# A fused two-layer graph network on one core: four edits at the seams between its stages

## The chip, the cores and the metric

The kernel runs on one core of a Trainium2 chip. A core has a matrix engine (TensorE, PE in the profile; its weight loads are PEld), a vector engine (VectorE, DVE), a scalar engine (ScalarE, ACT), a general engine (GpSimd, POOL), and SyncE (SP), which here issues almost all transfers between main memory and the on-chip memory. Each engine works through its own list of instructions in order; semaphores hold it back until what it reads is there. The metric is the device time in microseconds. Three runs of the kernel before took 2126.36, 2128.33 and 2132.01 us; the median, 2128.33 us, is the time before.

## The reference

There are 64 graphs of 256 nodes with 256 features, each with an adjacency matrix. Two layers follow each other, both with a layer norm and a ReLU at their input and a residual sum at their output.

```python
# layer 0
adj_hat = adj + eye; d = sum(adj_hat) ** -0.5
x = x + relu((d * adj_hat * d) @ h @ W.T + b)          # h = relu(layernorm(x))
# layer 1, h = relu(layernorm(x)) again
c = relu(bn1(conv1(h)))                                # 1 tap: a product with a 256 x 256 matrix
x_conv = relu(bn2(conv2(c)) + h)                       # 17 taps along the nodes
s = h @ w_se.T + b_se                                  # 3 columns
A = exp(-|s_n - s_m|^2) * adj
x_nmp = A @ relu(h @ w_msg.T + b_msg)
r, z, n = GRU gates of (concat(x_conv, x_nmp), h)
x = x + (1 - z) * n + z * h
```

All values are 32-bit floats.

## The kernel before

**Stage one** is a loop over n = 0 .. 67, software-pipelined over the 64 graphs: in pass n it aggregates and projects graph n (`aggregate`, `project`: layer 0), turns the normed rows of graph n-2 (`turn_h`), makes its messages (`messages`) and its first convolution (`conv1`), turns the three columns of graph n-3 (`turn_cols`) and computes its `distance`, and passes the messages of graph n-4 (`pass_messages`). Loads of `x` and `adj` come for two graphs at a time. Between these PE steps stands `beat(us)`: it runs the evictions and element-wise steps that are due (`after(k, ...)` puts a step off by k beats) and issues paced work of the long convolution, so much per microsecond of PE work. The wrappers `pe`, `act`, `vec` and `pool` keep the written order on these four engines. Transfers on SP are ordered by the scheduler and can be issued earlier than they are written.

In the profile, tiles are named: `ag`/`aggT` aggregation, `o`/`pre`/`x` projection and layer 0's sum, `ht`/`h2T` turned rows, `ms`/`mso`/`cols` messages and columns, `c`/`c1o` first convolution, `st`/`L`/`R`, `di`/`e`/`aT` distance and its mask, `nm`/`xnT` passed messages. `st` on DVE are moments of rows.

**Items.** Extra PE work is spread over the loop by `item()`, called up to eight times a pass. `pace` is a pair: what a call adds, and the credit it starts from; an item runs when the credit reaches 1. The 17-tap convolution is done with spectra: 48-point transforms of windows of the nodes, products per frequency, inverse transforms. First come its **filters**: at the end of pass 8 the turned taps are loaded into tiles `tp` (`filter_load`), and 32 items (`filter_part`) each make four products `fs` of 17 rows and 72 columns, in four banks of the PSUM memory, on four strips of 32 rows of the array; they are evicted to `fo` and stored as `wfd`. While filters run, only two of the eight calls count (`item(True)`), so two sets run a pass. When the list is empty, `conv_start` begins the convolution of the first 16 graphs: 32 `spectrum` items (`df` in the profile), then 24 `product` items (`y`), and the inverse transforms as paced work on POOL, DVE and ACT (`Xf`, `scr`, `hr`).

**Stage two** begins after the loop. PSUM is handed out anew: banks `ta`, `tc` and two `n` are first written by a product of the identity with a bias row `brzB`, so that later products add to what is there; then ACT copies the real biases in (`bank_of`). For each group q of 16 graphs, `turn_outputs` turns the convolution's outputs (`yt`, evicted to `xcT`), the spectra of the next group are computed (`spectrum`, which loads its next tile `h1l`), and then `gates` works on one graph after the other, with the `product`s of the next group between its parts. `wf_load` fetches the filters of one frequency part to one of eight tiles `wf` (WF = 8).

The lines that the change touches:

```python
            if 2 <= n <= B + 1:
                conv1(n - 2)
...
                    pace[:] = FILTER / 2, -5.0
...
    for tag, bufs in (("ta", 1), ("tc", 1), ("n", 2)):
        for k in range(bufs):
            t = ps_gate.tile([P, 2 * D], FP, tag=tag, name=f"first_{tag}_{k}", bufs=bufs)
            pe.matmul(t, ident, brzB, start=True, stop=True)
```

Of the kernel before, what the change touches and what calls it, by code (L numbers as in the profile page):

```python
# [11 lines left out]
FP = mybir.dt.float32  # L12
# [173 lines left out]
def gnn_kernel(  # L186
# [10 lines left out]
    B, N, D = x.shape  # L197
    P = 128
# [5 lines left out]
    NG = 16  # L204
# [6 lines left out]
    def scratch(name, shape):  # L211
# [17 lines left out]
    ident = const.tile([P, P], FP, tag="ident", name="ident")  # L229
# [4 lines left out]
    brzB = const.tile([P, 2 * D], FP, tag="brzB", name="brzB")  # L234
# [6 lines left out]
    pe, act, vec, pool = (  # L241
        Pinned(tc, e) for e in (nc.tensor, nc.scalar, nc.vector, nc.gpsimd)
    )
# [3 lines left out]
    def after(beats, go):  # L247
        due.append([beats, go])

    def come_due():  # L250
        now = []
        for d in list(due):
            d[0] -= 1
            if d[0] < 0:
                now.append(d[1])
                due.remove(d)
        for go in now:
            go()
# [59 lines left out]
    WF = 8  # L318

    def wf_load(n):  # L320
        if n < len(PARTS):
            u, k = PARTS[n]
            cv.wf[n] = wf = cv.stream.tile(
                [P, DC, D], FP, tag="wf", name=f"wf_{cv.q}_{u}_{k}", bufs=WF
            )
            nc.sync.dma_start(wf, wf_d[3 * u + k].rearrange("(c p) d -> p c d", c=DC))
# [217 lines left out]
    with ExitStack() as one:  # L544
# [11 lines left out]
        def beat(us):  # L556
            come_due()
            paced.issue(*(k * us for k in share))
# [442 lines left out]
        def own_bank(tag, k, bias):  # L1001
            width = bias.shape[2]
            shape = [P, NB, 512] if tag == "ms" else [P, NB, D]
            own[tag] = t = ps_own.tile(shape, FP, tag=tag, name=f"{tag}_{k}")
            act.copy(t[:, :, :width], bias.broadcast_to([P, NB, width]))

        def to_rows(g, tag, wT):
            s, t = st[g], own.pop(tag)
            for nb in range(NB):
                for cc in range(DC):  # L1010
                    pe.matmul(
                        t[:, nb, : wT.shape[2]], s["hT"][:, cc, nb * P : (nb + 1) * P],
                        wT[:, cc, :], start=False, stop=(cc == DC - 1), skip_group_check=True,
                    )
            return t

        def conv1(g):
            t = to_rows(g, "c1", w1T)

            def keep():  # L1020
                h1 = work.tile([P, NB, D], FP, tag="c1", name=f"c1o_{g}")
                act.activation(h1, t, AF.Relu)
                nc.sync.dma_start(h1_d[g].rearrange("p (c d) -> p c d", c=NB), h1)
            after(1, keep)
            if g + 1 < B:
                after(2, lambda: own_bank("c1", g + 1, b1B))
# [90 lines left out]
        t = ps_own.tile([P, NB, 512], FP, tag="ms", name="first_ms")  # L1117
        for nb in range(NB):
            pe.matmul(t[:, nb, :], ident, full, start=True, stop=True)
        t = ps_own.tile([P, NB, D], FP, tag="c1", name="first_c1")  # L1120
# [18 lines left out]
        pace = [0.0, 0.0]  # L1139
# [35 lines left out]
        FILTER, SPECTRA, PRODUCTS = 2, 5, 3  # L1175
        filtering = []
        for n in range(B + 4):
            even, odd = n % G == 0, n % G == 1
            if filtering and not items:
                filtering.clear()  # L1180
                while due:
                    beat(0.0)
                conv_start()
            if even and n + 2 * G < B:
                after(3, lambda n=n: load(n + 2 * G))
            if 2 <= n <= B + 1:
                turn_h(n - 2)
            beat(0.4)
            item()
            if n < B:  # L1190
                aggregate(n)
                if odd and n + 1 < B and n > 0:
                    after(2, lambda n=n: factors(n + 1))
                    for r in range(NR):
                        after((5, 7, 8, 9)[r], lambda r=r, n=n: layer0_in(n + 1, (r,)))
                if even and n + G < B:
                    after(4, lambda n=n: degrees(n + G))
                if odd and n + 3 < B:
                    for r in (0, 2):
                        after(3 + r // 2, lambda r=r, n=n: row_moments(n + 3, (r, r + 1)))  # L1200
            beat(1.7)
            item()
            if 3 <= n <= B + 2:
                turn_cols(n - 3)
            beat(0.2)
            if n + 1 < B:
                turn_adj(n + 1)
            beat(0.4)
            item()
            if n >= 4:  # L1210
                pass_messages(n - 4)
            beat(1.7)
            item(True)
            if 2 <= n <= B + 1:
                messages(n - 2)
            beat(1.7)
            item()
            if 3 <= n <= B + 2:
                distance(n - 3)
            beat(0.6)  # L1220
            item()
            if n < B:
                project(n)
            beat(1.7)
            item(True)
            if 2 <= n <= B + 1:
                conv1(n - 2)
            beat(1.7)
            item()
            if n == 0:  # L1230
                small_turns()
                turn_part(wmT, nat_wm, 0, D, "wm")
                T(WI, 0)()
                L(WI, 4)()
                own_bank("ms", 0, bmB)
            if n == 1:
                small_shift()
                turn_part(w1T, nat_w1, 0, D, "w1", scale=sc[:, 0:DC])
                beat(0.4)
                own_bank("c1", 0, b1B)  # L1240
                T(WI, 2)()
                L(WH, 0)()
            if n >= 2 and later:
                for go in later.pop(0):
                    go()
                if not later:
                    while due:
                        beat(0.0)
                    prep_stack.close()
                    spec_stack = ExitStack()  # L1250
                    spec = spec_stack.enter_context(tc.tile_pool(name="spec", bufs=1))
                    tab = spec.tile([P, 3 * UNITS], FP, tag="tab", name="tab")
                    nc.sync.dma_start(tab, nc.inline_tensor(filter_table(), name="tab_c").ap())
                    tp = {k: filter_load(k) for k in range(2)}
                    filtering.append(True)
                    pace[:] = FILTER / 2, -5.0
                    items.extend(
                        lambda k=k, j=j: filter_part(k, j) for k in range(4) for j in range(QC // 8)
                    )
# [8 lines left out]
    ps_gate = ctx.enter_context(tc.tile_pool(name="ps_gate", bufs=2, space=PSUM))  # L1268
# [222 lines left out]

    LEAD, PER = 3, 6

    for tag, bufs in (("ta", 1), ("tc", 1), ("n", 2)):
        for k in range(bufs):
            t = ps_gate.tile([P, 2 * D], FP, tag=tag, name=f"first_{tag}_{k}", bufs=bufs)
            pe.matmul(t, ident, brzB, start=True, stop=True)
    ready["ta"], ready["tc"] = bank_of("ta"), bank_of("tc")
    for nb in range(NB):
        ready["n", nb] = bank_of("n")  # L1500
# [1 line left out]
    for q in range(1, GROUPS + 1):  # L1502
        share[:] = 0.6, 0.6, 0.3
        ld = gate_inputs(q - 1, 0)
        paced.drain()
        xcT = big.tile([P, DC, P, OUT], FP, tag="xcT", name=f"xcT_{q}")
        turn_outputs(xcT)
        for go in gate_parts(ld, xcT):
            go()
        todo = []  # L1510
        if q < GROUPS:
            conv_begin(q)
            for k in range(WF):
                wf_load(k)
            for g in range(NG):
                for cb in range(DC):
                    spectrum(g, cb)
            for u in range(1, AHEAD):
                sums(u)
            todo = [lambda u=u: product(u) for u in range(UNITS)]  # L1520
            for _ in range(LEAD):
                todo.pop(0)()
        for g in range(NG):
            share[:] = (0.42, 0.55, 0.3) if todo else (0.51, 0.62, 0.3)
            between = [todo.pop(0) if todo else lambda: None for _ in range(PER)]
            ahead, nxt = None, None
            if g + 1 < NG:
                ahead = gate_inputs(q - 1, g + 1)
                nxt = gate_parts(ahead, xcT)
            gates(ld, between, nxt)  # L1530
            ld = ahead
            if q + 1 < GROUPS and g >= NG - H1:
                h1_load(q + 1, g - NG + H1)
# [34 lines left out]
```

## Time and profile before

| What | Value |
|---|---|
| median of three runs | 2128.33 us |
| profiled execution, its own time | 2127.08 us |
| its span, first to last instruction | 2125.3 us |
| PE busy | 2070.2 us, 97% of the span |
| DVE, ACT, POOL busy | 1415.8, 1018.1, 1098.4 us |
| mean granted clock of PE | 0.99 |
| first filter products | from 144.3 us |
| last product of stage one | 878.1 to 881.9 us |
| first turned outputs of stage two | 888.4 us |

The page's rows give an engine, an operation, its output and inputs by tile name, their shapes, a count, busy time and mean duration, and then the idle time of the engine ahead of these instructions with what ended it. Nearly all rows name line 102, which is the wrapper that records every operation, so rows are told apart by their tiles. In the view of waits, each line has the waiting engine and tile, what it waited for, and total, count and longest. In the timeline a line has start, duration, engine, operation, tiles, and in brackets the idle time before it. The clock is the share of full speed that PE was granted.

### The profile page before, as it was taken

Reading aid. Unit: us, or ns where it says so; the run is one execution under the profiler, and the core shown is the slowest. Engines: PE = TensorE matmul, PEld = TensorE weight load, DVE = VectorE, ACT = ScalarE, POOL = GpSimd, SP = SyncE. Lnnn points to the kernel's source line nnn. Section 1 sums busy time; section 2 is a strip of 40 time slices with the busy share of each in tenths; the row PEclk is TensorE's granted clock in tenths of the full one; section 3 lists DMA queues with packets and bytes.
Section 4 is the critical chain, followed back from the end, with each engine's and each line's share of the span. In section 5 each row is a group of like instructions: output and inputs, shape, how many; then the busy total and the mean of one; then the engine's idle time right before and its main releaser. Section 6 shows DMA issues by size and latency. Waiting matters only on the chain. (4 is left out here: it accounts for less than half of the span.)

```text
span 2125.3 us, 31287 instructions
## 1 busy us (share of the span) xinstructions
PE 2070.2 (97%) x9977; PEld 1741.0 (82%) x9977; DVE 1415.8 (67%) x3207; ACT 1018.1 (48%) x2203; POOL 1098.4 (52%) x1309
## 2 busy tenths in 40 slices
PE   7989999999999999999999999999999999999998
PEld 6866666888888888688888888888888888888887
DVE  6545656544588998515989924989933889964444
ACT  4856666666456676532234442233452234343333
POOL 4333323334675555327766716766725767644343
PEclk9999999999999999999999999999999999999999
DMA  8696777756766554556533446533355523322231
GB/s 289 229 250 213 226 221 231 260 174 187 238 214 211 181 173 156 178 177 194 169 105 113 136 149 198 184 109 111 113 155 180 176 85 123 112 81 92 90 100 60
DMA packets 292442, 352.86 MB, mean 166 GB/s; under 512 B 19475, under 2 KB 232102, under 8 KB 291622
## 3 DMA queue, kind: packets, MB, share of 16 engines
q1 hardware_dynamic: 291664, 346.26, 51.7%
q0 software_dynamic: 288, 4.46, 0.6%
q8 instruction: 80, 1.31, 0.3%
q14 instruction: 84, 0.69, 0.1%
q10 hardware_dynamic: 326, 0.14, 0.0%
HBM read 224.43 MB, written 126.35 MB: 165 GB/s over the span
## 5 line engine op out<-in xcount | busy, mean ns | idle before, releaser
L102 DVE TENSOR_TENSOR Xf<-y,k 128x256 f32<-128x256 f32 x184 | 69.1, 416 | 182.8 <-PE y L102 180.5
L102 DVE SCALAR_TENSOR_TENSOR Xf<-Xf 128x256 f32<-128x256 f32 (+1 forms) x248 | 183.9, 756 | 6.5 <-ACT Xf L102 5.4
L102 PE MATMUL ta<-T,S 128*128 128x256 f32 x768 | 186.6, 379 | 0.0
L102 PE MATMUL y<-wf,Xf 128*128 128x256 f32 x768 | 182.4, 380 | 1.7 <-DVE Xf L102 1.4
L102 POOL TENSOR_TENSOR aT<-e,adjT 128x512 f32<-128x512 f32 x64 | 82.3, 1286 | 187.3 <-ACT e L102 187.3
L102 POOL TENSOR_TENSOR rz<-u,p 128x256 f32<-128x256 f32 x64 | 47.8, 747 | 245.0 <-ACT u L102 245.0
L102 ACT ACTIVATE rz<-rz 128x512 f32<-128x512 f32 x128 | 80.2, 627 | 184.0 <-DVE rz L102 181.0
L102 PEld LDWEIGHTS y<-wf,Xf 128*128 128x128 f32 x768 | 144.4, 190 | 24.4 <-DVE Xf L102 2.6
L102 PEld LDWEIGHTS ta<-T,S 128*128 128x128 f32 x768 | 145.9, 190 | 19.8
L102 PE MATMUL n<-wiT,hx 128*128 128x256 f32 x512 | 152.3, 379 | 0.0
L102 DVE SCALAR_TENSOR_TENSOR h2l<-rz,h2l 128x256 f32<-128x256 f32 x128 | 104.4, 816 | 53.6 <-POOL h2l L102 53.6
L102 POOL TENSOR_TENSOR rs<-ve,mhalf 128x2 f32<-128x2 f32 (+1 forms) x65 | 46.9, 722 | 172.6 <-DVE nm L102 167.2
L102 POOL TENSOR_TENSOR xs<-Xf 128x256 f32<-128x256 f32 x92 | 70.9, 776 | 125.4 <-ACT Xf L102 63.4
L102 PE MATMUL o<-w0T,aggT 128*128 128x256 f32 x512 | 129.0, 395 | 5.6 <-ACT aggT L102 5.6
L102 POOL TENSOR_TENSOR adjH<-adjT,eye 128x512 f32<-128x512 f32 x64 | 82.0, 1282 | 96.5 <-ACT adjT L102 96.2
L102 PE MATMUL n<-whT,hx 128*128 128x256 f32 x512 | 131.4, 379 | 0.0
L102 PE MATMUL n<-wiT,xcT 128*128 128x256 f32 x512 | 131.4, 379 | 0.0
L102 PE MATMUL ms<-wmT,h2T 128*128 128x259 f32 x512 | 124.7, 386 | 2.8 <-DVE h2T L102 2.8
L102 PE MATMUL nm<-aT,mso 128*128 128x256 f32 x512 | 123.2, 384 | 4.2 <-POOL aT L102 3.4
L102 PE MATMUL ag<-adjH,hs 128*128 128x256 f32 x512 | 121.7, 380 | 4.8 <-POOL adjH L102 3.4
L102 PE MATMUL c<-w1T,h2T 128*128 128x256 f32 x512 | 125.9, 390 | 0.0
L102 PEld LDWEIGHTS o<-w0T,aggT 128*128 128x128 f32 x512 | 93.4, 192 | 35.8 <-issue 15.9
(185 smaller groups left out, 5339.3 us busy)
## 6 DMA issues: line engine op xcount, KB each, us to landing
wf<-wfd SPq DMA_DIRECT2D x284, 256.0 KB
wfd<-fo SPq DMA_DIRECT2D x32, 576.0 KB
x2d<-x SPq DMA_DIRECT2D x64, 256.0 KB
h2d<-h SPq DMA_DIRECT2D x64, 256.0 KB
hTd<-h2T SPq DMA_DIRECT2D x64, 256.0 KB
h1d<-c1o SPq DMA_DIRECT2D x64, 256.0 KB
xnd<-xnT SPq DMA_DIRECT2D x64, 256.0 KB
h1l<-h1d SPq DMA_DIRECT2D x64, 256.0 KB
```

The costliest lines, as they stand in the source:

```text
L102: return self.tc.keep_in_program_order(getattr(self.engine, op)(*args, **kwargs))
```

## The change

Four edits. The filter products start from a credit of -7 instead of -5, two calls later, which is one pass of the loop. The first convolution of the last graph (63) is made in pass 66, after the distance of that graph, instead of pass 65. The four gate banks are first written by four products of 32 rows of the identity, each on its own strip of the array, instead of four products with all 128 rows. In stage two the eight first filter tiles of a group are asked for beside the last eight spectra instead of ahead of all of them.

```diff
@@ stage one, pass n @@
-            if 2 <= n <= B + 1:
+            if 2 <= n <= B:
                 conv1(n - 2)
+            elif n == B + 2:
+                conv1(B - 1)
@@ start of the filters, end of pass 8 @@
-                    pace[:] = FILTER / 2, -5.0
+                    pace[:] = FILTER / 2, -7.0
@@ start of stage two @@
-    for tag, bufs in (("ta", 1), ("tc", 1), ("n", 2)):
-        for k in range(bufs):
-            t = ps_gate.tile([P, 2 * D], FP, tag=tag, name=f"first_{tag}_{k}", bufs=bufs)
-            pe.matmul(t, ident, brzB, start=True, stop=True)
+    for r, tag in enumerate(("ta", "tc", "n", "n")):
+        t = ps_gate.tile([P, 2 * D], FP, tag=tag, name=f"first_{r}", bufs=1 + (tag == "n"))
+        at = slice(32 * r, 32 * (r + 1))
+        pe.matmul(t, ident[at, :], brzB[at, :], start=True, stop=True)
@@ stage two, group q @@
-            for k in range(WF):
-                wf_load(k)
             for g in range(NG):
+                if g >= NG - WF:
+                    wf_load(g - NG + WF)
                 for cb in range(DC):
                     spectrum(g, cb)
```

## The prediction

> **What bounds the kernel now.** First the page: TensorE (PE) is busy for 97% of the span, so only its idle stretches and its slow stretches can be won.
>
> ```profile
> PE 2070.2 (97%) x9977; PEld 1741.0 (82%) x9977; DVE 1415.8 (67%) x3207; ACT 1018.1 (48%) x2203; POOL 1098.4 (52%) x1309
> ```
>
> Then the view of waits for PE (us in total, times, longest):
>
> ```profile
> PE fs L102 <- ACT e L102: 9.4, 1, 9.4
> ...
> PE nm L102 <- POOL aT L102: 3.4, 2, 3.0
> ...
> PE df L102 <- DMA h1l<-h1d: 1.4, 3, 0.9
> ...
> PE first_ta L102 <- ACT xnT L102: 0.7, 1, 0.7
> ```
>
> These four waits lie where the change works. The windows around them (us, busy time of PE, PEld, DVE, ACT, POOL, then granted clock, DMA share, GB/s) show that idleness is not the whole price: after it PE runs at half clock.
>
> ```profile
> 145.40:154.80 9.40, 0.01 (x2) 0.00 (x0) 3.64 (x15) 1.50 (x4) 0.00 (x0) 0.74 0.97 315
> 154.80:160.10 5.30, 5.25 (x11) 3.12 (x12) 3.10 (x10) 2.80 (x6) 2.28 (x3) 0.50 0.68 211
> ...
> 875.10:878.10 3.00, 0.00 (x0) 0.00 (x0) 2.90 (x4) 1.99 (x6) 2.30 (x4) 0.80 0.77 259
> 878.10:882.60 4.50, 3.78 (x8) 2.52 (x8) 3.72 (x6) 0.59 (x1) 3.31 (x3) 0.50 0.27 78
> 882.60:888.00 5.40, 5.37 (x8) 2.31 (x9) 0.00 (x0) 1.01 (x3) 0.01 (x1) 0.58 0.51 143
> ```
>
> Last, the timeline before the first filter products, to see who really is late:
>
> ```profile
> 139.78 0.39 SPq L822 DMA_DIRECT2D x<-in_x_dram  x1
> ...
> 144.33 1.08 PE L102 MATMUL fs<-tp,tab 17*72 17x512 f32 x4
> ...
> 150.92 0.43 DVE L102 BATCH_NORM_STATS2 st<-x 128x6 f32<-128x256 f32 x1 [13.10 <-DMA x<-in_x_dram]
> ...
> 153.07 0.16 DVE L102 COPY cols<-ms 128x24 f32<-128x24 f32 x1
> 153.26 0.60 ACT L102 ACTIVATE mso<-ms 128x512 f32<-128x512 f32 x1 [11.70 <-DVE cols L102]
> ...
> 154.42 0.65 ACT L102 ACTIVATE e<-di 128x256 f32<-128x256 f32 x2
> ...
> 154.85 2.25 PE L102 MATMUL fs<-tp,tab 17*72 17x512 f32 x4 [9.44 <-ACT e L102]
> 154.96 0.60 ACT L102 ACTIVATE hs<-x,nmr,rsd 128x256 f32<-128x256 f32 x1
> ```
>
> The filter products wait for PSUM banks that ACT's `e` must read out; ACT stands behind `mso`, `mso` behind DVE's `cols`, and `cols` behind the row moments of an `x` tile issued at 139.78 and there at 150.92. The tap tiles `tp` delay it: ten loads issued from 124.45 to 131.92, and DMA is 0.96 busy at 136 GB/s from 130 to 145.4.
>
> [...] a filter set, four products of 17 rows, holds PE for 1.02 to 1.05 us between `o` and `c`. [...] a DVE `Xf` of 256 columns takes 0.42 us alone and 1.48 beside a POOL sum. [...] `x` has a row of 0.39 us and 11.1 us until it is read.
>
> **Filters a graph later.** Up to 144.33 both programs are the same, the `x` and `tp` loads too, so `x` still lands at 150.9. PE now goes on with graph 11's `c` (1.8) and `ht` (0.4) to 146.6, and two of eight passes of `ag` of graph 12; the rest needs the second row block of `hs`. In the changed instruction order that stays behind `mso` and `e` on ACT: ready at 154.96 + 0.60 = 155.56. The wait moves to `ag` and is 9 us again. From 155.56 to 160.12 the clock is half as before: six passes of `ag` at 0.43 (2.56), `st` and `at` (0.65 x 2 = 1.3), 0.7 of `nm`. Then at full clock 1.4 of `nm`, `ms` 1.95, `di` 0.64, `o` 1.92, one filter set 1.1: the next `c` starts at 167.1, against 172.15 before, where three sets were done. Two sets are owed: one after `o` (1.02 + 0.09) and one after `nm` (1.61 + 0.09), 2.8 together. Gain 5.05 - 2.8 = 2.3 us. One 3.41 us clock window more or less at half rate is 1.7 either way: 0.6 to 4.0.
>
> The sets' evictions `fo` and stores `wfd` move with them and are still issued before the first convolution starts. The later end of the filters delays the start of the first convolution by a graph too. Its products are PE work of the same sum; its transforms on DVE, POOL and ACT end nearer to the end of stage one: after the last `h2T` copy DVE has three more 512-wide steps (3 x 0.70 = 2.1 us). Those are in the next sum.
>
> **The joint of the stages.** `c` of graph 63 stood at 870.16 and covers PE's wait for `aT` of graph 62 (POOL 871.15 + 1.27 = 872.42; `nm` starts at 872.48). Moved, that wait is bare (1.8 us idle) and `nm` starts no earlier; `c` then covers 1.75 us of the wait for `aT` 63. The move itself is worth 0; its eviction and its `h1d` store come some 5 us later, and only the last group reads them. But POOL's residual sums now stand behind `aT` 63, so it starts at 875.95, not at 876.64, and is not slowed: done at 877.2 (878.09 before). `nm` 63 takes 877.3 to 879.1 at full clock (878.13 to 881.9 before), and its copy `xnT` ends at 880.0 (882.6).
>
> The four bank-setting products hold PE from 882.63 to 888.40, mostly at half clock: 5.8 us. As row tiles, by the filter set's row, 1.0: 880.0 to 881.1. Most of that is not gained, because the outputs' turning (`yt`) comes next. Its evictions into `xcT` reuse stage one's memory and wait for the landing of graph 63's `xnd` store. Before, that store was issued at 883.57, and `whT`, which waits for it, at 886.69: 3.1 us. In the changed SP order the store stands behind the load `hr_4`, which needs the sums of point 7. I put those at 882.1: ACT's two 0.4 us products at 877.5, DVE held by POOL's sums to 880.6, 0.4, and a sum of 1.0. Store 882.7, landing 885.8, first eviction 885.9 against 889.12. PE, with three banks, idles from 882 to 886.6, so half clock for one window; the turning then takes its 7.1 us (889.12 to 896.23) plus about 1.3 (a pair of banks is 1.7 us of PE then, against 1.0 us of evictions). `df` starts at 894.3, not 896.23: gain 1.9; bounds -1 (two half-clock windows, `nm` slow as well) and 3.3 (no half clock).
>
> Costed at nothing there: on POOL the weight difference `T` of `whT` now stands ahead of point 15's last sum. `whT` goes out at 885.9, lands 4.6 later (886.69 to 891.26 before) at 890.5, then 0.73 and 0.97: 892.2. Its last transposes come near 893.4; past that it costs us for us. `hr_12` moves between `h1l` loads 4 and 5 on SP and waits for that sum; load 5 waits for a buffer until about 899 anyway.
>
> **Filter tiles after h1.** No gain. In both instruction orders of SP these eight loads stand in stage one for the first group, some 150 rows ahead of `h1l_3`, and 80 to 90 rows ahead in later groups: the scheduler had hoisted them already. Bounds: the `df` waits are 1.4 us in all, so 0 to 1.4; below zero little, as products follow 13 us after.
>
> **Sum.** Profiled execution 2127.08 (span 2125.3 and 1.8 around it), 1.25 below the median 2128.33. 2127.08 - 2.3 - 1.9 = 2122.9; as a median 2124.1.
>
> **Rivals.** (1) The first wait vanishes: 9.44 idle and 5.3 us at half clock (2.65), with the joint's 1.9: 2114.3. For it: the wait stands at `fs`. Against: `ag` reads `hs` from the same stuck ACT. (2) The gains cancel in clock windows and a slower turning: 2128. For: half clock costs 1.7 per window, and new idle stretches appear at the joint. Against: nothing longer than before. (3) Slower: with the convolution a graph later, DVE's transforms collide with `h2T`. Place: 600 to 870 us, where DVE is 87 and 92% busy in two 100 us windows and eight PE waits from 730 to 866 sum to 4.3 us, 0.53 each. If each of some 25 graphs there had one, 13.3 us: 2128.3 + 9.0 - 4.2 = 2133.1. It decides once DVE's work per graph exceeds PE's 10.6 us; counted in the changed order with the rows' durations it stays between 9.2 and 10.9, as before.
>
> **How the numbers follow.** My case 0.65, own range 2120 to 2128.5; rivals 0.13, 0.10, 0.12. The range 2117 to 2132 leaves out rival 1 and half of rival 3. 0.3% is 6.4 us, about what a measurement of this kernel can tell from no change. Faster by more: rival 1 and a tenth from my case, 0.23; slower 0.07; same 0.70.
>
> **What would show it.** DVE `st` waits about 13 us for `x` again, and a PE wait of about 9 us at `ag` near 146.6 to 155.6 replaces that at `fs`. If that wait is under 5 us, rival 1 is right. Four `first` products within 2 us; then an idle gap of 4 us or more ahead of the later `yt`; `df` starting 6 to 8 us after the first `xcT`. SP issues `wf` and `h1l` in the same order. I am wrong at the joint if `yt` follows the products without a gap.

## The result, and the profile after

The changed kernel took 2121.47 us (median of six runs, 2119.73 to 2122.24) against 2128.35 for the kernel before, run beside it: a ratio of 0.9965, 95% interval 0.9955 to 0.9976. That is 0.35% less, or 6.9 us; the forecast median was 2124.1. The profiled execution after has a span of 2120.1 us (before: 2125.3). The page's first part:

```profile
PE 2067.2 (98%) x9977; PEld 1741.6 (82%) x9977; DVE 1412.2 (67%) x3207; ACT 1017.8 (48%) x2203; POOL 1099.2 (52%) x1309
```

The view of waits for PE after the change (total us, times, longest):

```profile
PE ag L102 <- ACT hs L102: 9.1, 2, 8.7
...
PE yt L102 <- ACT xcT L102: 4.6, 4, 4.0
...
PE nm L102 <- POOL aT L102: 2.4, 3, 1.8
...
PE first L102 <- ACT xnT L102: 0.7, 1, 0.7
```

The wait of 9.4 us at `fs` is now one of 8.7 at `ag`. A wait of 4.0 us ahead of `yt` is new. A line that the same view had before is gone:

```profile
PE fs L102 <- DVE pre L102: 2.0, 2, 1.0
```

These are two waits of 1.0 us of filter products for a bank that DVE's `pre` had still to read. The windows around the new waits, after the change (us, busy time of PE, PEld, DVE, ACT, POOL, then granted clock, DMA share, GB/s):

```profile
147.15:155.80 8.65, 0.00 (x0) 0.00 (x1) 4.41 (x17) 2.32 (x6) 0.46 (x1) 0.74 0.89 312
155.80:161.60 5.80, 5.80 (x17) 4.80 (x18) 3.15 (x12) 4.69 (x10) 2.25 (x4) 0.50 0.70 222
864.94:868.14 3.20, 1.11 (x7) 0.50 (x7) 2.92 (x7) 1.82 (x5) 1.53 (x1) 1.00 0.15 58
868.14:871.56 3.42, 3.42 (x8) 2.53 (x8) 1.23 (x4) 0.00 (x0) 0.00 (x0) 0.50 0.00 0
...
877.37:878.44 1.07, 1.07 (x8) 0.31 (x8) 0.97 (x3) 0.57 (x2) 0.38 (x2) 1.00 0.52 131
878.44:883.92 5.48, 1.53 (x16) 1.29 (x12) 5.20 (x8) 3.11 (x8) 2.84 (x3) 1.00 0.52 174
883.92:888.60 4.68, 4.68 (x26) 4.52 (x27) 2.28 (x4) 2.08 (x4) 0.54 (x1) 0.64 1.03 362
```

The reader sees the four bank products in 1.07 us (5.77 before), then PE busy for 1.53 of 5.48 us, then `yt` partly at half clock (0.64 on the mean); and, new, `nm` of graph 62 wholly at half clock (0.50) after a stretch in which PE was idle for 2.09 of 3.20 us. The timeline before the first wait, after the change:

```profile
131.68 0.54 SPq L784 DMA_DIRECT2D tp<-wtd  x1
140.62 0.39 SPq L822 DMA_DIRECT2D x<-in_x_dram  x1
...
151.11 0.43 DVE L102 BATCH_NORM_STATS2 st<-x 128x6 f32<-128x256 f32 x1 [13.13 <-DMA x<-in_x_dram]
...
153.45 0.60 ACT L102 ACTIVATE mso<-ms 128x512 f32<-128x512 f32 x1 [11.74 <-DVE cols L102]
...
155.80 1.65 PE L102 MATMUL ag<-adjH,hs 128*128 128x256 f32 x3 [8.65 <-ACT hs L102]
```

`x` is as late as before, and the same chain stands behind it. Milestones, as start times on PE in the two traces, before minus after: `c` after the wait 4.31 us, with two filter sets owed (not yet made, but made by then before the change); `di` of graph 20, 9.40; `di` of graph 50, when everything owed is done, 6.70; `di` of graph 62, 4.59; the first `df` of stage two, 4.44; the end, 5.25. So the wait alone did not earn the gain (4.31 less 2.8 owed is 1.5), and the joint earned nothing. Between graphs 13 and 20 something else came in. The trace of before shows it. Its timeline at one filter set:

```profile
239.89 1.08 PE L102 MATMUL fs<-tp,tab 17*72 17x512 f32 x4
240.00 0.48 DVE L102 SCALAR_TENSOR_TENSOR pre<-o,dis,b0B 128x256 f32<-128x256 f32 x1 [1.83 <-PE o L102]
...
241.44 0.47 DVE L102 SCALAR_TENSOR_TENSOR pre<-o,dis,b0B 128x256 f32<-128x256 f32 x1
...
241.96 1.08 PE L102 MATMUL fs<-tp,tab 17*72 17x512 f32 x4 [0.99 <-DVE pre L102]
...
242.97 0.48 PE L102 MATMUL c<-w1T,h2T 128*128 128x256 f32 x1
```

The third product of this set got the bank of the `o` just computed, which DVE's second `pre` had still to read, and PE's order held the fourth behind it. The set took 3.08 us (239.89 to 242.97) instead of 1.03, so 2.05 more. A second one does so at 296.7, and after it the clock was at half rate (0.50) from 300.06 to 303.47. Such a stretch is called a slow window below: this one lasts 3.41 us, others in the two traces 3.41, 6.83 or 10.24 where the span does not cut them off. With PE busy all through it, as here, it costs half its length, 1.7. That is 2 x 2.05 + 1.7 = 5.8 us, an estimate from these rows; the lead grew by 5.1 between graphs 13 and 20. After the change no set waits for `pre`.

At the joint, after the change (timeline):

```profile
868.14 3.67 PE L102 MATMUL nm<-aT,mso 128*128 128x256 f32 x8 [1.82 <-POOL aT L102]
...
877.37 1.14 PE L102 MATMUL first<-brzB,ident 32*128 32x512 f32 x8 [0.72 <-ACT xnT L102]
...
879.84 0.52 SPq L1100 DMA_DIRECT2D xnd<-xnT  x1
...
882.71 0.42 DVE L102 TENSOR_TENSOR Xf<-Xf,hr 128x256 f32<-128x256 f32 x1
883.18 1.26 ACT L102 ACTIVATE xcT<-yt,sh 128x512 f32<-128x512 f32 x2 [2.28 <-DMA xnd<-xnT]
...
883.92 2.33 PE L102 MATMUL yt<-ident,Xf 128*128 128x128 f32 x14 [3.95 <-ACT xcT L102]
```

The first `xcT` copy on ACT waited for the landing of the store of graph 63's rows, as forecast; DVE's sums ended at 883.13, nearly the same time.

### The profile page after: what moved, and what is told of

Read it like the earlier page. It is cut to its first block, busy times and chain, and to the rows that moved or that the text cites. A ratio compares the mean times of both kernels' runs of the same rounds, so it can differ in the third digit from the quotient of the medians.

```text
span 2120.1 us, 31280 instructions
## 1 busy us (share of the span) xinstructions
PE 2067.2 (98%) x9977; PEld 1741.6 (82%) x9977; DVE 1412.2 (67%) x3207; ACT 1017.8 (48%) x2203; POOL 1099.2 (52%) x1309
```

## The experiments

The theory formed from the two traces: the first edit gains because no filter set falls on a bank that `pre` still reads; the second and third cost a slow window each; the fourth does nothing. The rival is the prediction's own account: the moved wait for `x` earns about 2 us and the joint about 2.

### The edits one at a time

Each kernel is the kernel before with one edit of the four. The first and second:

```diff
-                    pace[:] = FILTER / 2, -5.0
+                    pace[:] = FILTER / 2, -7.0
```

> The kernel before with the first edit alone (filter products a pass later). Prediction's step: only the wait for x moves from `fs` to `ag`, gain 2.3 us (0.6 to 4.0), so a profiled execution near 2124.8. Theory formed from the two traces: the gain is larger, since two filter sets of the kernel before (at 239.9 and 296.7 us) waited 0.99 us each for a bank that DVE's `pre` had to read, and one of them was followed by a slow clock window (300.06 to 303.48); without them `di` of graph 48 comes 5 to 6.5 us earlier than before (it does so by 6.0 in the changed kernel), and 3 to 6 us are left at the end: 2121 to 2124. Rival: the two waits come back at other sets, then `di` of graph 48 is 1 to 3 us earlier. The PE wait at `ag` of 8 to 9 us near 147 to 156 is there in all cases.

```diff
-            if 2 <= n <= B + 1:
+            if 2 <= n <= B:
                 conv1(n - 2)
+            elif n == B + 2:
+                conv1(B - 1)
```

> The kernel before with the second edit alone (first convolution of graph 63 after its distance). Prediction's step: worth 0, since a bare wait of 1.8 us for `aT` of graph 62 is exchanged for cover of the wait for `aT` of graph 63. Theory formed from the two traces: the bare wait trips the slow clock, `di` of graph 63 and `c` run at half rate, 1 to 2 us slower up to `nm` of graph 63. In the order of this kernel the residual sums on POOL stay ahead of `aT` 63, so part of the loss can vanish in the wait for it: 0 to 2 us slower in all, `nm` of graph 62 starts within 0.3 us of where it did relative to `di` of graph 62. Rival: a gain of 1 us or more, because `c` fills the wait for `aT` 63 and the slow window before the gate banks' products goes.

The third (the four products of 32 rows) and the fourth (`wf_load` beside the last eight spectra) are the hunks of the change itself.

> The kernel before with the third edit alone (gate banks set by four products of 32 rows). The four `first` products take about 1 us in place of 5.8 in all cases. Prediction's step: the gain is bound by the landing of the store of graph 63's rows, which stood at about 886.65 us before against a first `xcT` eviction at 889.12, so 2.4 us at most, less half a slow window (1.7) after the new idle stretch: 0.7 to 2.4 us faster. Rival: nothing binds, all of 3.7 to 4.8 us is gained, and `yt` runs without an idle stretch of 2 us or more before it. Second rival: 0 or slower, since DVE's paced sums after 880 us hold up the evictions as well.

> The kernel before with the fourth edit alone (filter tiles asked for beside the last eight spectra). Prediction's step: 0, since the rows on SP stand in the same order as before: ratio 1 within 0.1%, waits of `df` for `h1l` about 1.4 us in all as before. Rival: up to 1.4 us faster, if these waits go.

| kernel | median us | ratio to before, 95% interval |
|---|---|---|
| first edit alone | 2119.19 | 0.9953, 0.9940 to 0.9965 |
| second alone | 2130.37 | 1.0005, 0.9998 to 1.0011 |
| third alone | 2128.74 | 0.9994, 0.9987 to 1.0001 |
| fourth alone | 2128.21 | 0.9995, 0.9986 to 1.0003 |

The kernel before beside them: 2129.34 (49 runs, 2126.39 to 2133.40). The first edit is the whole gain, 10.2 us, more than all four together have (6.9). `di` of graph 50 stood at 737.56 us, as in the changed kernel; the bank waits were gone; the wait at `ag` was 10.1 us. The expectation of 2121 to 2124 was too cautious, as at the joint this kernel's profile has no slow window at all (granted clock 1.00, and 23.78 us from `di` 62 to `df`; 26.70 before).

The second edit alone was neutral: in this kernel's POOL order `nm` of graph 63 starts 8.60 us after `di` of graph 62, as before, and the slow window that was expected after the bare wait is not there. The third alone had `first` in 2.0 us, at half clock, instead of 3.5 to 5.8; a gain above 2.8 us is excluded, and none is shown, which does not tell the expected 0.7 to 2.4 us from nothing. The fourth is within its interval of nothing, as forecast.

### What the second and third edit do beside the first

The changed kernel with the second edit undone:

```diff
-            if 2 <= n <= B:
+            if 2 <= n <= B + 1:
                 conv1(n - 2)
-            elif n == B + 2:
-                conv1(B - 1)
```

> The changed kernel with the first convolution of graph 63 put back ahead of its distance; the other three edits stay. Theory: the bare wait of 1.82 us for `aT` 62 goes, and with it the slow window 868.15 to 871.56, so `nm` of graph 63 starts near 872.9 as with the first edit alone, not at 874.66; what is left is that four short `first` products leave PE idle for 3 to 4 us until the first `xcT` copy, and a slow window during `yt`. `df` then starts at 888.5 to 890.5, against 891.79, and the time is 1 to 3 us less than the changed kernel's. Rival: the first `xcT` copy comes no earlier than 883.2, since DVE's sums and the store of graph 63's rows set it, and `df` stays within 0.5 us of 891.8.

The changed kernel with the third edit undone:

```diff
-    for r, tag in enumerate(("ta", "tc", "n", "n")):
-        t = ps_gate.tile([P, 2 * D], FP, tag=tag, name=f"first_{r}", bufs=1 + (tag == "n"))
-        at = slice(32 * r, 32 * (r + 1))
-        pe.matmul(t, ident[at, :], brzB[at, :], start=True, stop=True)
+    for tag, bufs in (("ta", 1), ("tc", 1), ("n", 2)):
+        for k in range(bufs):
+            t = ps_gate.tile([P, 2 * D], FP, tag=tag, name=f"first_{tag}_{k}", bufs=bufs)
+            pe.matmul(t, ident, brzB, start=True, stop=True)
```

> The changed kernel with the four long bank-setting products back; the other three edits stay. Theory: the first `xcT` copy is set by the landing of the store of graph 63's rows and by DVE's sums, so the long products (3.6 to 5.7 us in place of 1.07) only fill PE's idle stretch of 3.95 us before the later `yt`: the first copy stays within 0.5 us of 883.2, the slow window during `yt` goes or comes earlier, `df` starts within 2 us of 891.8 and the time is within 1.5 us of 2121.5. Rival (the third edit is worth its 2.5 to 4.7 us): 2.5 us or more slower than 2121.5.

Medians: 2120.26 with the second undone, 2121.50 with the third undone. The differences to 2121.47 are too small for the runs; the traces separate the stretches. With the second undone the first `xcT` copy came at 882.27 and `df` at 891.14, which neither expectation had; with the third undone `df` and the time stayed within 2 and 1.5 us of the changed kernel's, as expected. In us, by start times on PE:

| kernel (edits) | `di` 62 to `nm` 63 | to `first` | to the later `yt` | to `df` | sum |
|---|---|---|---|---|---|
| first edit alone | 8.05 | 2.71 | 6.54 | 6.48 | 23.78 |
| second undone (1, 3, 4) | 8.05 | 2.71 | 6.57 | 8.13 | 25.46 |
| third undone (1, 2, 4) | 9.70 | 2.72 | 6.54 | 6.45 | 25.41 |
| all four | 9.72 | 2.71 | 6.55 | 7.87 | 26.85 |

Two readings. The move of the convolution adds 1.65 us in the first column: PE waits for `aT` 62 with nothing to cover it, and `nm` 62 runs at half clock (0.50 from 868.14 to 871.56 in the changed kernel). The first column is 9.69 to 11.64 us in all four traced kernels that have the first and the second edit, and 8.05 in the three that have the first without the second. And the third column is the same to 0.03 us whether the bank products take 3.5 us or 1.07: the short ones earned nothing there, they only opened an idle stretch of 4 us in place of one of 1.5. What follows it, the fourth column, ran at a mean granted clock of 0.81 and 0.78 in the two kernels with short products, and at 1.00 in both with long ones. The windows of the later `yt`, first with the second edit undone:

```profile
883.01:891.14 8.13, 7.80 (x52) 7.08 (x53) 4.54 (x7) 4.20 (x7) 1.41 (x2) 0.81 1.00 368
```

and with the third undone:

```profile
883.43:889.88 6.45, 6.45 (x53) 5.50 (x53) 4.72 (x7) 4.27 (x7) 1.41 (x2) 1.00 1.04 370
```

The granted clock is 0.81 against 1.00, and 1.4 to 1.65 us more are spent. The two edits together account for the 3.07 us between the first and the last row of the table. Over several executions less of it is seen: medians 2119.2 against 2121.5, with intervals that overlap. Why was not shown. Nor is a fast joint assured without these edits: in the kernel with the first edit alone and `tp` put off (below), a slow window from 861.48 to 868.31 makes the same sum 26.05.

### What sets the first copy

The changed kernel with the store of graph 63's rows issued on ACT's queue:

```diff
-                nc.sync.dma_start(xn_d[g].rearrange("p (c n) -> p c n", c=DC), xn)
+                e = nc.scalar if g == B - 1 else nc.sync
+                e.dma_start(xn_d[g].rearrange("p (c n) -> p c n", c=DC), xn)
```

> The changed kernel, but the store of graph 63's rows is issued on ACT's queue, ahead of SP's rows that wait. Prediction's step: the first `xcT` copy waits for the landing of that store (issued 879.84, copy at 883.18); issued near 877.6, it lets the first copy on ACT begin up to 2.3 us earlier, the idle stretch of PE before the later `yt` falls from 3.95 to 1.7 us or more, and `df` starts 1 to 3 us earlier. Rival: DVE's paced sums (until 883.13) hold up DVE's half of the copies, so `df` starts less than 1 us earlier and the time is the same within 1 us.

2122.74 us, ratio 0.9969 (0.9957 to 0.9980): no gain. Its timeline says why:

```profile
877.67 0.34 ACTq L1101 DMA_DIRECT2D xnd<-xnT  x1
...
881.31 1.26 ACT L102 ACTIVATE xcT<-yt,sh 128x512 f32<-128x512 f32 x2
...
883.05 0.43 DVE L102 TENSOR_TENSOR Xf<-Xf,hr 128x256 f32<-128x256 f32 x1
...
883.48 2.25 DVE L102 TENSOR_SCALAR xcT<-yt,sh 128x512 f32<-128x512 f32 x3
883.79 0.33 SPq L1287 DMA_DIRECT2D whT<-whd  x1
...
890.32 0.72 POOL L102 TENSOR_TENSOR T<-whT 128x256 f32<-128x256 f32 x1 [7.66 <-DMA whT<-whd]
891.00 0.72 POOL L102 TENSOR_TENSOR Xf<-Xf,hr 128x256 f32<-128x256 f32 x1
...
891.78 0.55 PE L102 MATMUL yt<-ident,Xf 128*128 128x128 f32 x3 [2.41 <-POOL Xf L102]
```

The landing did bind ACT's first copy, which is 1.87 us earlier (881.31 against 883.18). But DVE's copy still waits for its paced sums, and then the step that the prediction had put down as hidden, `T` from `whT` ahead of the last sum on POOL, comes out: PE waits 2.41 us for that sum. Part of this is that `whT` took 6.5 us from issue to use here (883.79 to 890.32) and 4.6 in the changed kernel (883.43 to 888.07). `df` starts 27.09 us after `di` of graph 62, against 26.85. The prediction's step was half right, the rival was right that no time is gained, and a third wait stood behind both.

### Later, or only elsewhere on the banks

The first edit with one further pass of delay:

```diff
-                    pace[:] = FILTER / 2, -5.0
+                    pace[:] = FILTER / 2, -9.0
```

> The kernel before with the filter products two passes later (credit -9), where the changed kernel has them one pass later (-7). In its built order two filter sets again take a bank that `pre` reads, in passes 19 and 23. Theory (what counts is how the sets fall on the banks, not that they are later): two PE waits of about 1 us at `fs` for `pre` are back, near 270 and 325 us, and the gain of the first edit (10.2 us) falls to 1 to 6 us: 2123 to 2128. Rival (later is what counts): the time is within 2 us of 2119.2, or below.

2131.71 us, ratio 1.0010 (1.0004 to 1.0017): the whole gain is gone, and more than was expected. The waits of this kernel:

```profile
PE fs L102 <- DVE pre L102: 2.0, 2, 1.0
...
PE yt L102 <- DVE Xf L102: 1.7, 1, 1.7
```

The two bank waits are back (258.7 and 317.3 us), each with a slow window of 3.41 us after it. `di` of graph 50 stands at 740.92, 3.4 us later than with -7. At graph 48 the lead over the kernel before is 1.7 us, where -7 has 6.0. The other 10.4 us are lost at the joint, where `df` comes 34.20 us after `di` of graph 62 instead of 23.78: the convolution's tail on DVE ends later than PE needs it (first DVE copy into `xcT` at 894.04, 17.5 us after `nm` of graph 63; 8.5 in the changed kernel). So the time of this kernel is no measure of the bank waits alone; its trace up to graph 48 is a better one. "Later" is no gain in itself, and two passes later loses all of it at the joint.

### The wait for `x`

Five of the ten `tp` loads are put off. The edit, made on the changed kernel, then on the first edit alone, then on the kernel before:

```diff
-                    tp = {k: filter_load(k) for k in range(2)}
+                    tp = {0: filter_load(0)}
@@ filter_part, keep() @@
+                if k == 0 and j == 1:
+                    tp[1] = filter_load(1)
```

> The changed kernel, but the second tile of taps (five of the ten `tp` loads) is asked for after the second filter set, not with the first. Theory: `x` of the next pair of graphs stands behind these loads, and its lateness is the whole wait at `ag` (8.65 us). With half of them gone `x` lands 5 to 10 us earlier, the wait falls to 0 to 3.5 us, and the 2.9 us that PE lost at half clock after it shrink as well: 5 to 11 us less than the changed kernel's 2121.5, so 2110 to 2116. Rival: the load of `x` isn't held by them, the wait at `ag` keeps 7 us or more and the time stays within 2 us. Second rival: the moved loads delay the next pair's `x`, and a new wait of several us stands 14 to 28 us later.

> The kernel before with the first edit alone, and the second tile of taps asked for after the second filter set. If both theories hold (the gain of the change comes from the first edit, the other three give back about 2 to 3 us at the joint, and the rest of the wait at `ag` comes from the `tp` loads), this is the fastest of all: 5 to 11 us below the first edit alone (2119.2), so 2108 to 2114. Rival: the time equals that of the first edit alone within 2 us.

> The kernel before, with only the second tile of taps asked for after the second filter set; the filters keep their old place. It tells what the first edit is worth when there is no late `x` to wait for. Theory (the first edit gains by taking two filter sets off banks that DVE's `pre` has to read): both waits of 0.99 us for `pre` are still there, near 230 and 287 us, with slow windows after them, and the time is 5 to 9 us above the 2108.6 of the same kernel with the first edit: 2114 to 2118. Rival (the first edit gains by filling the wait for `x`, as the prediction had it): nothing is left for it, and the time is within 2 us of 2108.6.

| kernel | without | with `tp` put off | ratio to before, 95% interval |
|---|---|---|---|
| all four edits | 2121.47 | 2109.34 | 0.9905, 0.9890 to 0.9920 |
| first edit alone | 2119.19 | 2108.57 | 0.9905, 0.9891 to 0.9918 |
| kernel before | 2129.5 | 2115.25 | 0.9932, 0.9920 to 0.9944 |

The wait at `ag` is gone in full, with the slow clock after it (with the first edit alone and `tp` put off, PE waits 0.4 us for `hs` in all, and the granted clock is 1.00 from 143 to 157). The timeline with the first edit alone and `tp` put off:

```profile
126.57 0.64 SPq L784 DMA_DIRECT2D tp<-wtd  x1
129.54 0.39 SPq L824 DMA_DIRECT2D x<-in_x_dram  x1
...
139.60 0.43 DVE L102 BATCH_NORM_STATS2 st<-x 128x6 f32<-128x256 f32 x1 [2.23 <-DMA x<-in_x_dram]
```

`x` is read 11.5 us sooner than in the changed kernel (139.60 against 151.11), and 11.1 of them are its issue (129.54 against 140.62); from issue to use it takes 10 us in both. What the loads held up was SP's queue, more than the data on its way.

The third row decides between the two accounts of the first edit. With no late `x` there is no wait to fill, yet the first edit is still worth 6.7 us by the medians (2115.25 against 2108.57), 5.7 by the ratios, whose intervals don't meet. And the trace of the kernel before with `tp` put off has both bank waits, at 226.2 and 286.3, followed by slow windows of 6.83 and 3.41 us. Its view of waits and the first of these windows:

```profile
PE fs L102 <- DVE pre L102: 2.0, 2, 1.0
...
227.71:234.54 6.83, 6.83 (x20) 4.83 (x17) 3.66 (x10) 2.27 (x4) 0.90 (x2) 0.50 0.50 161
```

The two passes that hold the waits take 18.98 and 17.34 us from `di` to `di` (graphs 14 to 15 and 18 to 19), against 13.94 and 13.95 with the first edit: 8.4 us more, enough for the whole difference. With `x` late the first edit is worth 10.2 us, with `x` in time 6.7. The 3.5 us between them, uncertain by a few us, are the room that is left for the prediction's account. The first two kernels of this table are the fastest of all that ran, 12 us and more ahead of the changed kernel.

## Why the prediction was right or wrong

The forecast was 2124.1, with 2117 to 2132 as range, and 2121.47 lies in it. That the total came out near is in part luck: two errors of opposite sign met. Forecast: 2.3 from the filters and 1.9 from the joint. The traces: 4.59 by `di` of graph 62, -0.15 from there to `df`, and 0.81 after, 5.25 in all; the 0.81 was not traced to a cause.

**Filters a graph later: the mechanism right, the sum incomplete.** `x` was read at 151.11 (forecast 150.9), the wait moved to `ag`, `hs` was ready at 155.80 (155.56). `c` came at 167.84, not 167.1, as the clock was back at full rate at 161.59, not 160.12. That is 1.5 us, within the 0.6 to 4.0. What failed is the step "Gain 5.05 - 2.8 = 2.3 us": it priced all other sets alike before and after, at about 1.1. Two sets of before cost 3.08. The line for it, `fs` waiting for `pre`, 2.0 us in two waits, stood in the view of waits a few lines below the one that was read. The runs: 5.7 to 6.7 us of gain from the first edit where the wait for `x` doesn't exist, and, with the credit of -9, which brings the bank waits back, a lead of 1.7 us at graph 48 in place of 6.0.

**Waits from 730 to 866 us.** Costed at nothing outside rival 3. The eight waits sum to 5.33 us after, 4.27 before, and the lead fell from 6.70 (graph 50) to 4.59 (graph 62): so PE lost something there, 2.1 us and 1.1 of it in these waits, but far less than the 13.3 of rival 3. That the later convolution is the cause is likely, not shown.

**The joint: one step failed.** "The move itself is worth 0" took PE's bare wait for `aT` 62 as a wait only. A slow window followed it, 868.15 to 871.56, worth 1.7. Put on before's time (4.59 added), `nm` 63 starts at 879.25 against a forecast of 877.3: 1.95 late. Everything after it holds: from `nm` 63 to the first `xcT` 8.52 (forecast 8.6), from there to `df` 8.61 (8.4). The traces with the second or third edit undone show 1.65 and 1.4 as the two edits' costs; the medians, 1.2 and 0.0, do not confirm them.

**Bank products.** "Most of that is not gained" was right; in fact none was, and the idle stretch of 3.95 us that they left was followed by a slow window, 885.20 to 888.61, which the forecast had priced. The forecast's comparison was with a kernel before whose joint was slow (26.70); with the fourth edit alone the same code took 24.36. **`T` ahead of the last sum**: hidden, as forecast (the sum runs from 888.75 to 889.49, while PE is still turning); with the store on ACT's queue, where the turning is earlier and `whT` comes later, it was 2.41 us of PE time. **Filter tiles after `h1`**: worth 0, as forecast.

**Rivals.** Rival 1, the wait vanishing, did not happen, but its price was about right: putting the five loads off is worth 10.6 to 14.3 us in the three kernels (forecast 9.44 + 2.65 = 12.1). Rival 3, slower by collisions on DVE, came with one more pass of delay, and the place is the joint, not 600 to 870 us.

**What stays open.** Which way the banks fall was seen in the waits and in the order of the instructions; why the pool of banks gives the set that one at -5 and -9 and not at -7 was not traced.

## What to carry to other kernels

Read every wait of the moved kind, the small ones too: here two of 1 us, each holding the rest of a set behind it and followed by slow clock in five of the six cases traced, were worth more than one of 9 us that only changed places. Work that fills a wait set by something else (a store's landing, another engine's sums) earns nothing when it is made shorter: first ask what ends that wait. When a load is late, look first at what stands ahead of it in its queue: putting five issues off was worth more than all four edits.

## What the runs showed of the hardware

Slow clock came after idle stretches much shorter than a slow window too. In the kernel before the clock was at half rate from 149.88 to 160.12, 300.06 to 303.47 and 876.91 to 887.15; in the changed kernel from 151.35 to 161.59, 868.15 to 871.56 and 885.20 to 888.61: 3.41 us, or 10.24. One of them followed 1.82 and 0.27 us of idleness within 3.2 us (changed kernel, at 868.15), and a slow window of 6.83 us followed one stretch of 0.98 (kernel before with `tp` put off, at 227.71). And the same stretch need not do it. The first bank wait of the kernel before, 0.99 us, had no slow clock after it (1.00 from 160.12 to 300.06); the same wait with `tp` put off had (0.50 from 227.71 to 234.54). In the kernel before, ahead of `nm` 63 and during it:

```profile
875.10:878.13 3.03, 0.00 (x0) 0.00 (x0) 2.93 (x4) 1.99 (x6) 2.33 (x4) 0.80 0.76 256
878.13:881.91 3.78, 3.78 (x8) 2.52 (x8) 3.57 (x6) 0.00 (x0) 2.59 (x3) 0.50 0.24 74
```

and the same two stretches with the fourth edit alone:

```profile
877.66:880.69 3.03, 0.00 (x1) 0.00 (x1) 2.92 (x4) 1.99 (x6) 2.33 (x4) 1.00 0.78 254
880.69:882.68 1.99, 1.99 (x8) 1.44 (x8) 1.89 (x3) 0.00 (x0) 1.56 (x2) 1.00 0.48 144
```

3.03 us idle both times; half clock and 3.78 us for `nm` in one, full clock and 1.99 in the other. The instructions there are the same; what made the difference was not shown. The amount of idle time alone does not tell it either: in the kernel before, the 3.41 us ahead of the slow window at 300.06 had 0.99 us idle, while in the changed kernel 3.41 us with 1.83 idle (878.39 to 881.80) were followed by full clock until 885.20. The slow windows named above start whole multiples of 3.413 us apart within each trace (before, 44 and 169 of them; after, 210 and 5); why was not shown. A slow window of one profile is therefore no fixed price of an edit, and a difference of two profiles can carry some us of such windows: among the four kernels with the filters at -5 and `tp` in place, `di` of graph 30 stood anywhere from 459.99 to 464.16.
